# Two scan terms added on GpSimd before TensorE turns them, and a block's experts and biases summed in one PSUM bank

## The chip, the core and the metric

The kernel runs on one core of a Trainium2 chip. The core has five engines, each with an instruction queue of its own that runs in order: TensorE (PE, matmuls; its weight loads are listed apart as PEld), VectorE (DVE), ScalarE (ACT), GpSimd (POOL) and SyncE (SP), which here issues the DMAs of the main part. SBUF is the on-chip memory of 128 partitions; PSUM, in eight banks of 128x512 fp32, is where TensorE writes. The metric is the device time of one execution in microseconds, taken as the median of several runs.

## The reference

Two layers on four images of 128 channels and 64x64 pixels, all in fp32. Layer 0 is a hybrid of a local convolution and a Mamba scan, layer 1 is attention followed by a mixture of experts. The two parts that the change touches, cut to what matters:

```python
# layer 0, per image and channel group; N = 16 states, L = 4096 positions
dA  = jnp.exp(delta[..., None] * A)
dBu = delta[..., None] * Bm[:, :, None, :] * xin[..., None]
def step(h, inp):
    dA_t, dBu_t, C_t = inp
    h = dA_t * h + dBu_t
    y = jnp.einsum('bdn,bn->bd', h, C_t)      # a sum over the 16 states
    return (h, y)
...
y = ys + D_skip * xin
out = y * silu(z) @ out_proj_w.T

# layer 1, mixture of experts: 8 experts, the two best of each token
router_probs = softmax(x @ router_w + router_b)
top_p, top_i = top_k(router_probs, 2); top_p = top_p / sum(top_p)
expert_out = einsum('bnd,edc->bnec', x, expert_w) + expert_b
out = einsum('bnk,bnkc->bnc', top_p, take_along_axis(expert_out, top_i))
t = t + out
```

## The kernel before

An image is cut into 8 blocks of 512 positions, 32 blocks in all (b, i). Everything lies as 128 partitions by 512 positions. The scan of a block runs in two passes (p = 0, 1), each with 128 of the inner channels in the partitions, and a pass in 8 *units* of two states each (n = 0, 2, ... 14): 512 units. One scan instruction of VectorE carries both states of a unit, 1025 columns long.

The main loop (from line 1322) walks through *slots*, two to a unit; `END` is 1024. Its order of calls is the order of every engine's queue: `Queue` and `queued` (lines 450 to 467) chain each instruction behind the one before it on the same engine, which is why nearly all instructions carry line 467 in the profile; tiles tell them apart. What a unit does:

- In its even slot `driven` (line 799) multiplies the unit's B rows, broadcast by DMA from memory (`rows`), with `du` into `h` (VectorE, 128x1024), and `scan` runs the recurrence in place. ScalarE has made the decays `da` in the slots before (`decayed`).
- In its odd slot `read` (line 813) multiplies `h` with the C rows into `hc`, a tile of two buffers, 128x2x512: one half per state.
- The sum over the 16 states is made by TensorE: `turned_on` (line 824) transposes a half in four 128x128 pieces and accumulates into the PSUM tile `y`. The pieces wait in the deque `due` with a slot from which they may go: state 0 from the slot after the readout (three slots after it in the first unit of a pass), state 1 two slots after. They leave in the order in which they came. Behind the last unit of a pass, ScalarE copies `y` out (`yT`), `turned_back` transposes it back in the next slot, and `summed_up` gates it one slot later.

Beside this the loop issues, in every slot, one group of attention: four score matmuls (`sc`, from `attention`), two exponentials of 128x1024 on ScalarE (`pT`, `exponentials`) and, one slot later, eight matmuls with the values (`av`, `weighted`). There are 1024 groups; they begin when the first blocks are through layer 0, and the last of them run after slot 1024.

All other work lies in two *lanes*, X and Y: generators that are moved on by one `yield` twice a slot (`advance`, line 1216). Lane Y holds norms and convolution (`group_norm`, `first_norm`, `conv`; from the second image on the convolution's nine taps are VectorE's) and the projections of `inputs` (line 713). Lane X holds `closed` (the end of layer 0 and the projections of attention) and `finished` (line 1087: the end of attention, the router and the experts of one block). When the scan is over, lane Y takes blocks of `finished` too. Each lane has one PSUM bank, `work(lane)` (line 509). `inputs` uses both banks, and the set `held` with the entry "in" keeps another `inputs` away while it does. If an input is not ready when its rows are due, `until` (line 1246) moves the lanes on until it is.

`finished` computes the router, then `prT`: the eight weights of each token and, below, the same over the norm. For each pair of experts, `share` loads the weights' rows broadcast to all partitions by DMA, VectorE multiplies them with the tokens `xf` (128x1024), and TensorE applies the two experts (`ew`). In the version before, the bias term (`eb8` with `prT`) and each of the four pairs are separate results in the lane's bank, and VectorE adds them one by one into `res`, the first together with `xf`.

GpSimd has little to do: the powers `rs` (an inverse square root of 128x4), the products `shift` behind them, and small fills and copies at the rims of tiles. ScalarE's normalisation `xt` waits for `rs` and `shift`.

Of the kernel before, what the change touches and what calls it, by code (L numbers as in the profile page):

```python
# [24 lines left out]
NST = 16  # L25
DH = 32
NH = 4
NE = 8
# [8 lines left out]
def conv_mamba_attn_moe_kernel(ctx: ExitStack, tc: tile.TileContext, t: dict):  # L37
# [435 lines left out]
    def mm(out, lhsT, rhs, start=True, stop=True):  # L473
        tensor.matmul(out, lhsT=lhsT, rhs=rhs, start=start, stop=stop)
# [8 lines left out]
    def send(out, in_, slots=1):  # L483
        outgoing.append([slots, out, in_])
# [24 lines left out]
    def work(lane, shape=None):  # L509
        return ps_work.tile(shape or [P, BLK], F32, tag=f"work{lane}", name=f"ps_{lane}")  # L510

    def tmp(lane, name, shape=None):
        return side.tile(
            shape or [P, BLK], F32, tag=f"tmp{lane}", name=name, bufs=6 if lane == "X" else 4
        )
# [197 lines left out]
    def inputs(b, i, p):  # L713

        xn, pairs = xn_of[b, i], pairs_of[b, i]
        r = slice(DI * p, DI * p + DI)
        while held:
            yield
            yield
        held.add("in")  # L720
        ps = work("Y")
        summed(ps, [(inxc[:, j, :], pairs[:, p, 2 * j : 2 * j + BLK]) for j in range(2)])
        pz = work("X")
        mm(pz, inz[r, :], xn[r, 3 : 3 + BLK])
        yield
        xin = mix.tile([P, BLK], F32, name="xin", bufs=2)
        scalar.activation(xin, ps, AF.Silu, bias=cb)
        zs = mix.tile([P, BLK], F32, name="zs", bufs=4)
        scalar.activation(zs, pz, AF.Silu)
        yield  # L730

        pb = work("X")
        mm(pb[0:DI, :], wbc, xin)
        ps = work("Y")
        mm(ps, wdt, xin)
        yield
        held.clear()
        bc = tmp("Y", "bc")[0:DI, :]
        scalar.copy(bc, pb[0:DI, :])
        bcd = dram.tile([2, NST // 2, 2, 2 * BLK], F32, name="bcd", bufs=4)  # L740
        send(bcd.rearrange("c n k (m q) -> (c n k m) q", m=2), bc)

        e = tmp("Y", "e")
        scalar.activation(e, ps, AF.Abs, bias=dtb)
        scalar.activation(e, e, AF.Exp, scale=-1.0)
        ln = tmp("Y", "ln")
        scalar.activation(ln, e, AF.Ln, bias=1.0)
        delta = mix.tile([P, BLK], F32, name="delta", bufs=2)
        scalar.activation(delta, ps, AF.Relu, bias=dtb)
        yield  # L750
        yield

        du = mix.tile([P, BLK], F32, name="du", bufs=2)
        lost = du
        vector.tensor_scalar(lost, e, 1.0, -1.0, ALU.add, ALU.add)
        vector.tensor_sub(lost, e, lost)
        vector.tensor_add(ln, ln, lost)
        vector.tensor_add(delta, delta, ln)
        vector.tensor_mul(du, delta, xin)
        in_of[b, i, p] = xin, zs, delta, du, bcd  # L760
        done.add(("in", b, i, p))
        yield
# [324 lines left out]
    def finished(b, qb, lane):  # L1087

        q, u = divmod(qb, 2)
        td = kqv[b][3]  # L1090
        s = slice(qb * BLK, (qb + 1) * BLK)
        acc = side.tile([P, NT, C], F32, name="acc", bufs=2)
        aT, inv = tmp(lane, "aT"), tmp(lane, "inv")
        sync.dma_start(out=aT, in_=total[b, q][u, 0].rearrange("h d q -> (h d) q"))
        sync.dma_start(
            out=inv, in_=inverse[b, q][u][:, None, :].to_broadcast([NH, DH, BLK])
        )
        sync.dma_start(out=acc.rearrange("p j c -> p (j c)"), in_=td[:, s])
        yield
        yield  # L1100
        yield
        vector.tensor_mul(aT, aT, inv)
        yield
        ps = work(lane, [P, NT, C])
        for j in range(NT):
            mm(ps[:, j, :], aT[:, j * P : (j + 1) * P], wp)
        yield
        vector.tensor_add(acc, ps, acc)
        rs = spread(lane, acc)
        yield  # L1110
        ps = transposed(lane, acc)
        yield
        xf = tmp(lane, "xf")
        scalar.copy(xf, ps)
        yield
        ps = work(lane, [P, NT, NE])
        for j in range(NT):
            mm(ps[:, j, :], xf[:, j * P : (j + 1) * P], rw)
        wide = [P, NT, NE]

        def routed(name, n=NE):
            return small.tile([P, NT, n], F32, name=f"{name}{lane}", bufs=1)

        yield

        both = routed("both", 2 * NE)
        pr = routed("pr")
        vector.tensor_mul(pr, ps, rs[:, :, None].to_broadcast(wide))
        vector.tensor_add(pr, pr, rb[:, None, :].to_broadcast(wide))
        m = routed("m", 1)  # L1130
        vector.tensor_reduce(m, pr, AX.X, ALU.max)
        vector.tensor_sub(pr, pr, m.to_broadcast(wide))
        yield
        yield
        scalar.activation(pr, pr, AF.Exp)
        yield
        yield

        revb = rev[:, None, :].to_broadcast(wide)

        def largest(src, tag):
            top, f, pick = routed(f"top{tag}", 1), routed(f"f{tag}", 1), routed(f"pick{tag}")
            vector.tensor_reduce(top, src, AX.X, ALU.max)
            vector.tensor_tensor(pick, src, top.to_broadcast(wide), ALU.is_equal)
            vector.tensor_mul(pick, pick, revb)
            vector.tensor_reduce(f, pick, AX.X, ALU.max)
            vector.tensor_tensor(pick, pick, f.to_broadcast(wide), ALU.is_equal)
            return top, pick

        top1, pick1 = largest(pr, 1)  # L1150
        rest = routed("rest")
        vector.scalar_tensor_tensor(rest, pick1, -2.0, pr, ALU.mult, ALU.add)
        top2, pick2 = largest(rest, 2)
        vector.tensor_add(pick1, pick1, pick2)
        vector.tensor_mul(pr, pr, pick1)
        vector.tensor_add(top1, top1, top2)
        vector.reciprocal(top1, top1)
        vector.tensor_mul(both[:, :, 0:NE], pr, top1.to_broadcast(wide))
        vector.tensor_mul(both[:, :, NE:], both[:, :, 0:NE], rs[:, :, None].to_broadcast(wide))
        yield  # L1160

        ps = work(lane)
        for j in range(NT):
            tensor.transpose(ps[0 : 2 * NE, j * P : (j + 1) * P], both[:, j, :], ident)
        yield
        prT = tmp(lane, "prT")[0 : 2 * NE, :]
        scalar.copy(prT, ps[0 : 2 * NE, :])
        shares = dram.tile([NE, BLK], F32, name=f"shares{lane}")
        send(shares, prT[NE:, :])
        yield  # L1170

        def share(e):

            if lane == "X":
                w = side.tile([P, 2, BLK], F32, name="share", bufs=3)
            else:
                w = mix.tile([P, 2, BLK], F32, tag="rows", name="share", bufs=4)
            sync.dma_start(
                out=w.rearrange("p k q -> p (k q)"),
                in_=shares[e : e + 2].rearrange("e q -> (e q)")[None].to_broadcast([P, 2 * BLK]),  # L1180
            )
            return w


        ps = work(lane)
        mm(ps, eb8, prT[0:NE, :])
        yield
        res = tmp(lane, "res")
        vector.tensor_add(res, ps, xf)
        yield  # L1190
        ahead = deque(share(e) for e in (0, 2))
        yield
        yield
        for e in range(0, NE, 2):
            if e + 4 < NE:
                ahead.append(share(e + 4))
            yield
            w = ahead.popleft()
            if e:
                vector.tensor_add(res, res, ps)  # L1200
            vector.tensor_mul(w, w, xf[:, None, :].to_broadcast([P, 2, BLK]))
            yield
            ps = work(lane)
            for u in range(2):
                mm(ps, ew[:, e + u, :], w[:, u, :], u == 0, u == 1)
        yield
        vector.tensor_add(res, res, ps)
        send(out[b][:, s], res, 2)
        yield


# [86 lines left out]
    groups = attention_groups()  # L1298
    units = [(b, i, p, n) for b, i in blocks for p in range(2) for n in range(0, NST, 2)]
    END = 2 * len(units)  # L1300

    rows, due, closing, y_of = {}, deque(), deque(), {}
    h_of, slot = {}, 0
# [18 lines left out]
    while (  # L1322
# [23 lines left out]
        if unit and odd:  # L1346
            hc = read(h, rows.pop((at, 1)))
            late = 2 * (unit[3] == 0)
            due.append((slot + 1 + late, unit, 0, hc[:, 0, :], False))
            due.append((slot + 2, unit, 1, hc[:, 1, :], ends(unit)))  # L1350
        advance("Y", False)
        while closing and closing[0][0] <= slot:
            summing = turned_back(*closing.popleft()[1:])
# [133 lines left out]
```

## Time and profile before

| what | us |
|---|---|
| median of three runs | 5234.72 (5234.31 to 5243.44) |
| the profiled execution, whole | 5221.24 |
| its span, first to last instruction | 5219.4 |
| PE busy | 4743.5 (91%) |
| PEld busy | 2300.7 (44%) |
| DVE busy | 3834.5 (73%) |
| ACT busy | 3749.8 (72%) |
| POOL busy | 423.5 (8%) |
| mean granted TensorE clock | 0.958 of full speed |

Busy time is the time in which an engine ran at least one instruction, with register, branch, semaphore and DMA-issuing instructions left out. Over the whole span it mixes three phases: a start in which the first blocks go through layer 0, a long middle in which scan and attention run side by side, and an end in which attention and experts of the last image are left. A line of the groups reads: source line, engine, operation, out<-in by the program's names, shapes, count, then busy time in us and mean ns of one, then idle time of the engine just before them and what ended it. A line of the timeline reads: start, length, engine, line, operation, names, shapes, count.

The chain of work that ended last, followed back from the last instruction, shares the span like this: PE 55%, DVE 18%, ACT 13%, DMA 6%, issue 5%, POOL 2%; its largest single parts are `av` on PE with 23%, `sc` on PE with 13%, the experts' `ps_X` on PE with 8%, `h` on DVE with 6%, and `y` on PE with 5%.

### The profile page before, as it was taken

How to read it: one execution, taken by the hardware profiler on the slowest of the kernel's cores; microseconds unless marked ns; L12 is line 12 of the kernel's file. 1: busy time of each engine (PE TensorE's matmuls, PEld its weight loads, DVE VectorE, ACT ScalarE, POOL GpSimd, SP SyncE). 2: the span in 40 equal slices, each digit the busy share in tenths (PEclk: the TensorE clock that was granted, in tenths of full speed). 3: DMA queues.
4: the chain of work that ended last, by engine and by line, in shares of the span. 5: the costliest groups of instructions: out<-in, count | busy, mean ns of one | idle time of the engine just before them, and what ended most of it. 6: DMA issues, size and time to landing. Idle time of an engine off the chain costs nothing.

```text
span 5219.4 us, 62693 instructions
## 1 busy us (share of the span) xinstructions
PE 4743.5 (91%) x20704; PEld 2300.7 (44%) x20704; DVE 3834.5 (73%) x5809; ACT 3749.8 (72%) x5701; POOL 423.5 (8%) x483
## 2 busy tenths in 40 slices
PE   4566898999999999899999999999999999999997
PEld 2333444444444444444444444444444444443443
DVE  4888767777788877888788877888788877751332
ACT  3456787788777777688887787788777787756543
POOL 1111101100000000001000000000000001000000
PEclk8677999999999999899999999999999999999998
DMA  3556667767776667767766667767766666754542
GB/s 96 188 186 202 206 215 247 232 231 238 244 231 218 227 227 243 238 232 246 260 230 231 224 223 230 262 227 259 259 236 227 215 230 226 263 181 153 184 134 72
DMA packets 451694, 1131.62 MB, mean 217 GB/s; under 512 B 51985, under 2 KB 135330, under 8 KB 451362
## 3 DMA queue, kind: packets, MB, share of 16 engines
q1 hardware_dynamic: 450194, 1126.74, 64.3%
q8 instruction: 166, 2.72, 0.2%
q14 instruction: 166, 1.36, 0.1%
q10 hardware_dynamic: 1168, 0.80, 0.1%
HBM read 967.12 MB, written 143.39 MB: 213 GB/s over the span
## 4 chain that ended last, share of the span: by engine, by line
PE 55%; DVE 18%; ACT 13%; DMA 6%; issue 5%; POOL 2%; SPq 1%; DVEq 0%; ACTq 0%; POOLq 0%
PE av L467 23%; PE sc L467 13%; PE ps_X L467 8%; DVE h L467 6%; PE ps_Y L467 5%; PE y L467 5%; ACT pT L467 4%; ACT L467 3%; DMA ks<-kd 2%; DVE hc L467 2%; ACT xt L467 1%; ACT e L467 1%; DMA rows<-bcd 1%; DVE stX L467 1%; POOL rsX L467 1%
## 5 line engine op out<-in xcount | busy, mean ns | idle before, releaser
L467 ACT ACTIVATE pT<-sc 128x1024 f32<-128x1024 f32 x2048 | 1984.8, 1023 | 940.1 <-PE sc L467 938.4
L467 PE MATMUL av<-pT,v 128*64 128x512 f32 x8192 | 1998.3, 609 | 12.4 <-DVE avs L467 12.4
L467 PE MATMUL sc<-qs,ks 128*128 128x512 f32 x4096 | 1296.1, 436 | 64.4 <-DMA ks<-kd 32.7
L467 DVE TENSOR_TENSOR_SCAN h<-da,state,h 128x1025 f32<-128x1025 f32 x512 | 1204.2, 2352 | 90.0 <-ACT h L467 56.2
L467 PEld LDWEIGHTS sc<-qs,ks 128*128 128x128 f32 x4096 | 701.3, 190 | 793.3 <-ACT pT L467 261.7
L467 PEld LDWEIGHTS av<-pT,v 128*64 128x64 f32 x8192 | 499.5, 137 | 844.4 <-issue 813.8
L467 ACT ACTIVATE da<-delta,amat 128x512 f32<-128x512 f32 x1024 | 743.0, 730 | 1.9
L467 PE MATMUL y<-ident,hc 128*128 128x128 f32 x4096 | 626.6, 284 | 64.9 <-DVE hc L467 64.9
L467 DVE TENSOR_TENSOR hc<-rows,h 128x1024 f32<-128x1024 f32 x512 | 624.2, 1219 | 16.1 <-PE y L467 5.9
L467 DVE TENSOR_TENSOR h<-rows,du 128x1024 f32<-128x1024 f32 x512 | 623.4, 1218 | 14.2 <-DMA rows<-bcd 13.7
L467 PEld LDWEIGHTS y<-ident,hc 128*128 128x128 f32 x4096 | 520.6, 147 | 235.7 <-issue 83.9
L467 ACT ACT_TABLE_LOAD x319 | 409.3, 1283 | 19.5 <-DVE zs L467 14.3
L467 POOL TENSOR_TENSOR rsX<-rsX,mhalf 128x4 f32<-128x4 f32 x92 | 203.8, 2216 | 2524.6 <-DVE rsX L467 2440.5
L467 POOL TENSOR_TENSOR rsY<-rsY,mhalf 128x4 f32<-128x4 f32 x100 | 130.4, 1304 | 2071.0 <-DVE shiftY L467 1560.3
L467 DVE TENSOR_TENSOR avs<-av,prev 128x512 f32<-128x512 f32 x96 | 66.1, 689 | 252.9 <-PE av L467 238.3
L467 PE MATMUL ps_X<-share,w_ew 128*128 128x512 f32 x432 | 215.5, 622 | 8.7 <-DVE share L467 8.5
L467 ACT ACTIVATE xt<-ps_Y,shiftY,rsY 128x128 f32<-128x128 f32 x380 | 143.8, 469 | 106.4 <-POOL shiftY L467 99.0
L467 DVE TENSOR_TENSOR share<-share,xf 128x1024 f32<-128x1024 f32 x128 | 155.9, 1218 | 15.6 <-DMA share<-sharesX 9.9
L467 ACT COPY state<-h 128x2 f32<-128x2 f32 x448 | 88.7, 198 | 93.5 <-DVE h L467 93.5
L467 DVE SCALAR_TENSOR_TENSOR cm<-y,w_fc1w,cm 128x512 f32<-128x512 f32 x192 | 142.8, 744 | 3.4
L467 PE MATMUL ps_Y<-pairs,inxc 128*128 128x512 f32 x256 | 129.2, 629 | 15.6 <-DMA pairs<-xn 10.3
L467 PEld LDWEIGHTS ps_X<-share,w_ew 128*128 128x128 f32 x432 | 73.6, 190 | 146.8 <-issue 98.5
(254 smaller groups left out, 3455.8 us busy)
## 6 DMA issues: line engine op xcount, KB each, us to landing
rows<-bcd SPq DMA_DIRECT2D x1024, 512.0 KB
ks<-kd SPq DMA_DIRECT2D x192, 512.0 KB
qs<-qd SPq DMA_DIRECT2D x161, 512.0 KB
share<-sharesX SPq DMA_DIRECT2D x108, 512.0 KB
v<-vd SPq DMA_DIRECT2D x192, 256.0 KB
ks<-kd SPq DMA_DIRECT2D x128, 256.0 KB
avd<-avs SPq DMA_DIRECT2D x96, 256.0 KB
prev<-avd SPq DMA_DIRECT2D x96, 256.0 KB
```

The costliest lines, as they stand in the source:

```text
L467: return lambda *args, **kw: queued(op(*args, **kw))
```

## The change

Two parts.

**The scan's terms.** From slot `ALONE` on (64, the end of the second block), GpSimd adds the two halves of `hc` in place, right behind `read` in the order of issue, and one group of four transposes turns the sum into `y`, two slots after the readout (three in the first unit of a pass). Before slot 64 all stays as it was.

**The experts.** `finished` no longer adds each result on VectorE. The bias matmul opens an accumulation in the lane's bank just ahead of the first pair of experts, the eight expert matmuls go on in the same bank, and one addition at the end makes `res` from it and `xf`. Since the bank of lane X is now in use from the first pair to the last, `finished` in lane X waits while `held` is not empty, and then enters "mix", which keeps `inputs` away until `res` is made.

```diff
--- before.py
+++ after.py
@@ -734,7 +734,7 @@
         ps = work("Y")
         mm(ps, wdt, xin)
         yield
-        held.clear()
+        held.discard("in")
         bc = tmp("Y", "bc")[0:DI, :]
         scalar.copy(bc, pb[0:DI, :])
         bcd = dram.tile([2, NST // 2, 2, 2 * BLK], F32, name="bcd", bufs=4)
@@ -1182,30 +1182,34 @@
             return w
 
 
-        ps = work(lane)
-        mm(ps, eb8, prT[0:NE, :])
-        yield
-        res = tmp(lane, "res")
-        vector.tensor_add(res, ps, xf)
+        yield
         yield
         ahead = deque(share(e) for e in (0, 2))
         yield
         yield
+        while lane == "X" and held:
+            yield
+            yield
+        if lane == "X":
+            held.add("mix")
+        ps = None
         for e in range(0, NE, 2):
             if e + 4 < NE:
                 ahead.append(share(e + 4))
             yield
             w = ahead.popleft()
-            if e:
-                vector.tensor_add(res, res, ps)
             vector.tensor_mul(w, w, xf[:, None, :].to_broadcast([P, 2, BLK]))
             yield
-            ps = work(lane)
+            if e == 0:
+                ps = work(lane)
+                mm(ps, eb8, prT[0:NE, :], True, False)
             for u in range(2):
-                mm(ps, ew[:, e + u, :], w[:, u, :], u == 0, u == 1)
-        yield
-        vector.tensor_add(res, res, ps)
+                mm(ps, ew[:, e + u, :], w[:, u, :], False, e + u == NE - 1)
+        yield
+        res = tmp(lane, "res")
+        vector.tensor_add(res, ps, xf)
         send(out[b][:, s], res, 2)
+        held.discard("mix")
         yield
 
 
@@ -1298,6 +1302,7 @@
     groups = attention_groups()
     units = [(b, i, p, n) for b, i in blocks for p in range(2) for n in range(0, NST, 2)]
     END = 2 * len(units)
+    ALONE = NB // 2 * NST
 
     rows, due, closing, y_of = {}, deque(), deque(), {}
     h_of, slot = {}, 0
@@ -1346,8 +1351,12 @@
         if unit and odd:
             hc = read(h, rows.pop((at, 1)))
             late = 2 * (unit[3] == 0)
-            due.append((slot + 1 + late, unit, 0, hc[:, 0, :], False))
-            due.append((slot + 2, unit, 1, hc[:, 1, :], ends(unit)))
+            if slot < ALONE:
+                due.append((slot + 1 + late, unit, 0, hc[:, 0, :], False))
+                due.append((slot + 2, unit, 1, hc[:, 1, :], ends(unit)))
+            else:
+                gpsimd.tensor_add(hc[:, 0, :], hc[:, 0, :], hc[:, 1, :])
+                due.append((slot + 2 + late // 2, unit, 0, hc[:, 0, :], ends(unit)))
         advance("Y", False)
         while closing and closing[0][0] <= slot:
             summing = turned_back(*closing.popleft()[1:])
```

## The prediction

> **What bounds the kernel now.** I read the busy time by stretches first, then the groups, then the waits, then the order of time. The 1024 slots of the scan begin at about 100 us and their last readout starts at 4608 us; the 33rd of the 512 readouts (slot 64, from where the change adds) starts at 316 us. So three stretches matter (columns: length, then PE, PEld, DVE, ACT, POOL busy, granted clock, DMA share, GB/s):
>
> ```profile
> core 0: us, PE busy (x) PEld busy (x) DVE busy (x) ACT busy (x) POOL busy (x), PEclk, DMA share, GB/s
> 310.00:520.00 210.00, 144.03 (x559) 77.27 (x559) 175.12 (x236) 119.43 (x220) 26.13 (x26) 0.80 0.59 198
> 520.00:4600.00 4080.00, 3862.55 (x17302) 1880.81 (x17303) 3262.27 (x4739) 3186.23 (x4877) 350.04 (x381) 0.98 0.70 235
> 4600.00:5219.00 619.00, 576.22 (x2284) 246.07 (x2280) 177.10 (x470) 308.63 (x345) 12.61 (x13) 0.96 0.42 140
> ```
>
> TensorE is busy 95% of the middle stretch (3863 of 4080), VectorE 80%, ScalarE 78%. Before 520 us attention has hardly begun and VectorE leads (175 of 210); after 4600 us TensorE alone finishes the last image. The waits agree: the engines behind TensorE wait for it, and it waits little (us in total, times, longest).
>
> ```profile
> ACT pT L467 <- PE sc L467: 938.4, 661, 9.5
> DVE avs L467 <- PE av L467: 238.3, 62, 17.3
> PE y L467 <- DVE hc L467: 64.9, 21, 9.0
> ```
>
> The groups that the change touches (busy us, mean ns of one, idle before):
>
> ```profile
> L467 PE MATMUL y<-ident,hc 128*128 128x128 f32 x4096 | 626.6, 284 | 64.9 <-DVE hc L467 64.9
> L467 DVE TENSOR_TENSOR hc<-rows,h 128x1024 f32<-128x1024 f32 x512 | 624.2, 1219 | 16.1 <-PE y L467 5.9
> L467 DVE TENSOR_TENSOR h<-rows,du 128x1024 f32<-128x1024 f32 x512 | 623.4, 1218 | 14.2 <-DMA rows<-bcd 13.7
> L467 DVE TENSOR_TENSOR res<-res,ps_X 128x512 f32<-128x512 f32 x108 | 73.7, 682 | 51.9 <-PE ps_X L467 51.5
> ```
>
> Before its 512 `h` products VectorE idles 14.2 us in all: each starts right behind whatever went before, so a delay there is passed on until VectorE next idles, before `avs` for example.
>
> **Transposes removed.** Of 512 units 480 lose one of two groups of four transposes: 1920 instructions. What a group takes of TensorE's order:
>
> ```profile
> 2511.45 1.47 PE L467 MATMUL y<-ident,hc 128*128 128x128 f32 x12
> 2512.85 1.94 PE L467 MATMUL av<-pT,v 128*64 128x512 f32 x8
> ...
> 2515.75 0.60 PE L467 MATMUL y<-ident,hc 128*128 128x128 f32 x4
> 2516.28 1.94 PE L467 MATMUL av<-pT,v 128*64 128x512 f32 x8
> ```
>
> Four of them move `av` back by 2516.28 - 2515.75 = 0.53 us; twelve take 1.40, so 0.47 for four; by busy time it is 4 x 626.6/4096 = 0.61. I take 0.53, the group as it stands between two others, and keep 0.47 and 0.61. The middle stretch holds 449 readouts (29 fall before 520 us, 2 after 4600), so TensorE sheds 449 x 0.53 = 238 us there.
>
> **GpSimd's additions.** 480 of them, 128x512, two inputs in SBUF. No row shows this form. The nearest (minimum/median/maximum ns):
>
> ```profile
> L467 POOL TENSOR_TENSOR shiftY<-shiftY,rsY x95: 200/249/1910, 43.6 to 4408.5; 128x4 f32<-128x4 f32 x95
> L467 POOL COPY y<-y x28: 235/240/1155, 50.2 to 4224.3; 128x64 f32<-128x64 f32 x28
> L467 POOL COPY xn<-xn x28: 180/182/2246, 156.4 to 4409.6; 128x3 f32<-128x3 f32 x28
> ```
>
> From 3 to 64 columns a copy grows by 55 ns, 0.90 ns a column. Below: the fill of a 128x512 tile, `vst`, takes 0.54 us and reads nothing. Above: 235 ns for 64 columns, taken as all columns, makes 1.88 us for 512. Between, nearest in kind: 180 + 2 x 0.90 x 509 = 1.10 us, the copy's slope once for each input; I take that. POOL then works 480 x 1.10 = 528 us more and, 8% busy now, has room.
>
> The price is on VectorE. The maxima above are not work:
>
> ```profile
> 886.03 2.34 DVE L467 TENSOR_TENSOR_SCAN h<-da,state,h 128x1025 f32<-128x1025 f32 x1
> 886.45 1.91 POOL L467 TENSOR_TENSOR shiftY<-shiftY,rsY 128x4 f32<-128x4 f32 x1
> ```
>
> The shift product of 0.20 us, started inside the scan, ends at 888.36, as the scan does at 888.37: GpSimd is shut out while VectorE reads two operands from SBUF. No row shows the reverse, since its present operands are four columns. Lower bound of VectorE's loss per addition: 0; upper: the whole addition, 1.88. I take exclusion as mutual, so VectorE loses 1.10 where such an operation stands right behind the readout. Followed through VectorE's order from 470 us on, that is so behind 392 of 459 readouts (0.85), mostly the next unit's `h` product or a convolution tap; behind the others it idles or reads PSUM. Mean loss 0.85 x 1.10 = 0.94 us per unit.
>
> The Trainium skill, SBUF — State Buffer, section "SBUF: two separate sides", calls the port pair of VectorE and GpSimd an exclusive lock held for a whole instruction; the scan's row agrees for one direction, and by it the sum would be the one taken here. The rule against this change is in GPSIMD Engine Reference, "Engine selection": two-input elementwise work belongs on VectorE, GpSimd being 1.96 times slower. On a row of 0.69 us for a 128x512 product that is an estimate of 1.36 us, and by it the kernel would gain about 10 us only.
>
> **Waits added.** An addition waits for the readout; behind it on POOL stand the `rs` powers and `shift` products that ScalarE's `xt` waits for. TensorE waits for `xt` 22 times before a matmul; an addition is ahead or running for about 2.2 of the 9.1 us of a unit (4080/449), so 22 x 0.24 x 1.10 = 6 us; bounds 0 and 22 x 1.10 = 24. TensorE's own wait for the sum costs nothing: the group stands one slot (4.5 us) later than the first group did, which covers POOL's 1.10 and up to 2.35 behind a scan. Without that cover it would be those 3.45 us at each of the 21 waits shown, 72 us. For the first unit of a pass it stands as before, three slots behind the readout. The `hc` buffer comes free in the same slot as before.
>
> **Experts in one bank.** Four of five `res` additions per block go: 128 x 0.69 = 88 us of VectorE, some 60 of it before 4600 us (22 of 32 blocks), 1.0 us per 68 us; the ten later blocks find VectorE 71% idle: nothing. The bias matmul moves by some four slots, and shares, loads and yields stay in number and place. The hold: counted through the code's yields, a block's mixing lies at slots 11 to 17 of its 32, the input projections at 3 and 24 or, in an image's last block, 19; they touch once. Where they would meet, the input has three slots to spare. Zero; with that cover gone, one bunching of some slots, say 10 to 20 us.
>
> **Sum.** Cutting 520 to 4600 us into sixty stretches of 68 us and adding up the busiest engine of each gives 3871 us, 0.949 of the time; TensorE leads in 58. Per stretch (7.5 units) TensorE's work shrinks by 4.0 and VectorE's time grows by 7.5 x 0.94 - 1.0 = 6.0. Two of them:
>
> ```profile
> 2356.00:2424.00 68.00, 66.30 (x306) 31.84 (x304) 54.93 (x79) 58.53 (x91) 7.48 (x7) 1.00 0.79 263
> 3036.00:3104.00 68.00, 65.75 (x306) 32.47 (x304) 64.29 (x119) 49.77 (x83) 9.78 (x14) 1.00 0.68 229
> ```
>
> become 62.3 against 60.9, and 61.8 against 70.3, where VectorE takes over. It leads in 29 of the sixty; the maxima add up to 3765, at 0.949 that is 3968: -112 us. Before 520 us, where VectorE leads, 29 x 0.94 = +27. With POOL's +6: **-79 us**. The profiled execution (5219.4 us span, 5221.2 in all) becomes 5142; the median of the runs is 13.5 higher, so **5156 us**.
>
> **Rivals.**
> 1. *VectorE isn't held up*: lower bound of the loss, 0 to 0.46 per unit (an addition of 0.54). The maxima add up to 3650 to 3695, -233 to -186 in the middle, with the early cost -233 to -173, down to -263 at 0.61 a group: 4972 to 5062. For it: only POOL is seen waiting. Against: a shared path should stop either.
> 2. *VectorE becomes the bound, and it is slower*: the price is the addition's hold on VectorE behind the readout. With the early units the sum is zero at a loss of 1.2 us a unit, an addition of 1.4. At 1.60 (1.88 x 0.85) it is +104 in the middle and +46 early: 5385. For it: VectorE already leads in two stretches and readouts are followed at once; against: the copy's slope is far below.
> 3. *No effect*: the transposes hid under waits that stay. Against: TensorE idles 5%. It would end within 10 us, about 5235.
>
> **Chances.** Forecast (0.46 to 1.15 lost a unit, 5060 to 5220) 0.50; rival 1 0.20; rival 2 0.22; rival 3 0.08. A measurement of this kernel tells about 0.2% (10 us) from no change: faster 0.70, same 0.08, slower 0.22. The range runs from 4985, most of rival 1, to 5270, the cheap part of rival 2. The forecast's own is 5060 to 5220.
>
> **What would show it.** 2176 `y` transposes of `hc`, some 333 us busy; a POOL group `hc` of 480, near 1.1 us where VectorE idles, longer behind a scan; `h`, scan or the next product late or longer by about 1 us behind readouts; 32 `res` additions; TensorE below 93% of the middle stretch. I am wrong if an addition takes 1.4 us or more of VectorE, or if its rows don't move at all.

## The result, and the profile after

The changed kernel takes 5249.7 us (median of 20 runs, 5235.7 to 5254.8), the kernel before beside it 5238.4 (5231.5 to 5249.8): a ratio of 1.0021, 95% interval 1.0014 to 1.0028. The forecast was 5156, with its own range at 5060 to 5220; the change is 11 us slower, and all that it was to save is gone. The profiled execution has a span of 5246.9 us, 27.5 more than before. The stretches that the prediction used, in the kernel after (length, then PE, PEld, DVE, ACT, POOL busy, granted clock, DMA share, GB/s; the last one is 27 us longer than before):

```profile
310.00:520.00 210.00, 126.02 (x428) 63.10 (x426) 188.95 (x234) 113.36 (x209) 74.22 (x53) 0.75 0.59 196
520.00:4600.00 4080.00, 3722.92 (x15400) 1687.02 (x15396) 3456.60 (x4613) 3176.91 (x4858) 1178.64 (x826) 0.96 0.70 233
4600.00:5246.00 646.00, 602.09 (x2410) 257.68 (x2408) 181.02 (x472) 330.78 (x377) 30.88 (x23) 0.97 0.43 146
```

TensorE is busy 91% of the middle instead of 95%, VectorE 85% instead of 80%, and the scan is no faster: its last readout starts at 4642 us instead of 4608. The scan's group on the page before, then the groups of the page after (busy us, mean ns of one, idle before):

```profile
L467 DVE TENSOR_TENSOR_SCAN h<-da,state,h 128x1025 f32<-128x1025 f32 x512 | 1204.2, 2352 | 90.0 <-ACT h L467 56.2
```

```profile
L467 PE MATMUL av<-pT,v 128*64 128x512 f32 x8192 | 2018.3, 614 | 25.4 <-DVE avs L467 25.0
L467 PE MATMUL sc<-qs,ks 128*128 128x512 f32 x4096 | 1320.1, 442 | 125.4 <-ACT pT L467 66.6
L467 POOL TENSOR_TENSOR hc<-hc 128x512 f32<-128x512 f32 x480 | 826.7, 1722 | 2352.1 <-DVE hc L467 2164.0
L467 DVE TENSOR_TENSOR_SCAN h<-da,state,h 128x1025 f32<-128x1025 f32 x512 | 1339.3, 2616 | 68.8 <-ACT h L467 33.9
L467 DVE TENSOR_TENSOR h<-rows,du 128x1024 f32<-128x1024 f32 x512 | 700.6, 1368 | 7.3 <-DMA rows<-bcd 7.2
L467 PE MATMUL y<-ident,hc 128*128 128x128 f32 x2176 | 354.8, 292 | 55.0 <-DVE hc L467 36.9
```

The change does what it says: 2176 transposes instead of 4096, 480 additions on GpSimd. The scan's mean went from 2352 to 2616 ns and the `h` product's from 1218 to 1368, though they compute what they did. The order of time of VectorE and GpSimd shows how:

```profile
3029.37 1.22 DVE L467 TENSOR_TENSOR h<-rows,du 128x1024 f32<-128x1024 f32 x1
3029.53 2.19 POOL L467 TENSOR_TENSOR hc<-hc 128x512 f32<-128x512 f32 x1 [3.66 <-DVE hc L467]
3030.69 3.18 DVE L467 TENSOR_TENSOR_SCAN h<-da,state,h 128x1025 f32<-128x1025 f32 x1
...
3051.09 1.35 POOL L467 TENSOR_TENSOR hc<-hc 128x512 f32<-128x512 f32 x1
3051.41 1.59 DVE L467 TENSOR_TENSOR ln<-ln,du 128x512 f32<-128x512 f32 x1
```

The first addition starts 0.16 us into the `h` product and takes 2.19 us, where the shortest of the 480 takes 1.255: it ends 1.13 us behind the product's end at 3030.59, as if it had hardly begun before. The scan, which starts 0.1 us behind that end, takes 0.83 us more than its 2.35. At 3051 a product of 0.69 us takes 1.59. Each engine holds the other up, as the prediction assumed. And TensorE's waits, two of the kernel before and then those after (us, times, longest); before, it also waited 45.9 us for `bothX` and 32.7 for `ks`:

```profile
PE ps_Y L467 <- ACT xt L467: 71.3, 22, 7.7
PE sc L467 <- ACT pT L467: 30.5, 91, 1.6
```

```profile
PE ps_Y L467 <- ACT xt L467: 87.8, 56, 7.7
PE ps_X L467 <- DVE bothX L467: 74.9, 27, 6.6
PE sc L467 <- ACT pT L467: 66.6, 156, 2.6
PE sc L467 <- DMA ks<-kd: 56.4, 24, 9.3
```

No new wait dominates; many small ones grew. Where the 27.5 us come from, with each moment of TensorE's order put down to the matmul that started last: `hc` transposes 566 to 318 us (-248), all other matmuls 4178 to 4295 (+117), idle 476 to 634 (+159).

### The profile page after: what moved, and what is told of

The parts are those of the page before. It is cut to its first block, busy times and chain, and to the rows that moved or that the text cites. A ratio compares the mean times of both kernels' runs of the same rounds, so it can differ in the third digit from the quotient of the medians.

```text
span 5246.9 us, 59811 instructions
## 1 busy us (share of the span) xinstructions
PE 4612.4 (88%) x18784; PEld 2103.2 (40%) x18784; DVE 4044.0 (77%) x5681; ACT 3756.0 (72%) x5701; POOL 1318.5 (25%) x963
## 4 chain that ended last, share of the span: by engine, by line
PE 41%; DVE 28%; ACT 13%; DMA 7%; issue 7%; POOL 2%; SPq 1%; DVEq 0%; ACTq 0%; POOLq 0%
PE av L467 17%; DVE h L467 12%; PE sc L467 10%; PE ps_X L467 6%; PE ps_Y L467 5%; ACT pT L467 4%; ACT L467 3%; DVE hc L467 3%; DMA ks<-kd 3%; PE y L467 2%; DVE cm L467 2%; ACT xt L467 2%; DMA rows<-bcd 1%; DVE stY L467 1%; DVE stX L467 1%
## 5 line engine op out<-in xcount | busy, mean ns | idle before, releaser
L467 PE MATMUL sc<-qs,ks 128*128 128x512 f32 x4096 | 1320.1, 442 | 125.4 <-ACT pT L467 66.6
L467 POOL TENSOR_TENSOR hc<-hc 128x512 f32<-128x512 f32 x480 | 826.7, 1722 | 2352.1 <-DVE hc L467 2164.0
L467 DVE TENSOR_TENSOR_SCAN h<-da,state,h 128x1025 f32<-128x1025 f32 x512 | 1339.3, 2616 | 68.8 <-ACT h L467 33.9
L467 PEld LDWEIGHTS sc<-qs,ks 128*128 128x128 f32 x4096 | 712.5, 193 | 876.4 <-ACT pT L467 388.1
L467 DVE TENSOR_TENSOR h<-rows,du 128x1024 f32<-128x1024 f32 x512 | 700.6, 1368 | 7.3 <-DMA rows<-bcd 7.2
L467 PE MATMUL y<-ident,hc 128*128 128x128 f32 x2176 | 354.8, 292 | 55.0 <-DVE hc L467 36.9
L467 PEld LDWEIGHTS y<-ident,hc 128*128 128x128 f32 x2176 | 292.4, 152 | 167.7 <-issue 61.0
L467 DVE SCALAR_TENSOR_TENSOR cm<-y,w_fc1w,cm 128x512 f32<-128x512 f32 x192 | 185.7, 967 | 3.4
L467 PE MATMUL ps_Y<-ident,xt 128*128 128x128 f32 x380 | 72.3, 322 | 87.9 <-ACT xt L467 87.8
```

Source lines behind the costliest of these rows:

```text
L467: return lambda *args, **kw: queued(op(*args, **kw))
```

## The experiments

Ratios are to the kernel before in the same comparison, with 95% intervals. Its medians there lie between 5234 and 5242 us, so a few us between two tables say nothing. Kernels that leave a term out, or count it twice, serve to measure alone.

**First set: the scan's part, taken apart.** Two by two: four or eight transposes a unit, with and without the addition, experts as before.

`e1_half_turned`, no addition, four transposes:

```diff
-                gpsimd.tensor_add(hc[:, 0, :], hc[:, 0, :], hc[:, 1, :])
                 due.append((slot + 2 + late // 2, unit, 0, hc[:, 0, :], ends(unit)))
```

> The scan part of the change without GpSimd's addition: from slot 64 on one group of four transposes a unit turns state 0 alone, so the second state of 480 units is left out of the sum; experts as before the change. Theory A (the transposes were worth their TensorE time, and the addition's hold on VectorE gives it back): 180 to 260 us below the kernel before, VectorE's scan back at 2352 ns mean. Theory B (the transposes were not on the path, something else paces the slots): less than 60 us below. Theory C (TensorE's clock falls when it has less to do and eats the gain): less than 100 us below, with a granted clock clearly under 0.95.

`e2_late_group`, no addition, eight transposes in one later group:

```diff
-                gpsimd.tensor_add(hc[:, 0, :], hc[:, 0, :], hc[:, 1, :])
-                due.append((slot + 2 + late // 2, unit, 0, hc[:, 0, :], ends(unit)))
+                due.append((slot + 2 + late // 2, unit, 0, hc[:, 0, :], False))
+                due.append((slot + 2 + late // 2, unit, 1, hc[:, 1, :], ends(unit)))
```

> Both states are turned as before, eight transposes a unit, but in one group at the later slot; no addition, experts as before. All theories that blame the addition: within 15 us of the kernel before. A rival (turning one slot later, in one lump, costs by itself): more than 25 us above.

`e3_turn_both`, `e2` with the addition kept:

```diff
+                gpsimd.tensor_add(hc[:, 0, :], hc[:, 0, :], hc[:, 1, :])
                 due.append((slot + 2 + late // 2, unit, 0, hc[:, 0, :], False))
                 due.append((slot + 2 + late // 2, unit, 1, hc[:, 1, :], ends(unit)))
```

> GpSimd adds as in the change, but both halves are turned in one late group of eight, so state 1 of 480 units is counted twice; experts as before. What the addition alone costs, against the kernel with the late group. Theory A: 150 to 260 us above it. Theory B (TensorE is not the bound, VectorE is hidden too): under 60 us above it.

`e4_terms_only`, the change without its edits to `inputs` and `finished`; on the changed kernel, in short:

```diff
-                mm(ps, eb8, prT[0:NE, :], True, False)
...
+                vector.tensor_add(res, res, ps)
```

> The scan part of the change alone, experts as before the change. If the experts' part brings what it takes off VectorE's path: 10 to 60 us above the changed kernel. If the experts' bank is what costs (the accumulation over five slots, the hold): below the changed kernel by 30 us or more.

| kernel | median us | ratio |
|---|---|---|
| e1 no addition, four | 5138.4 | 0.9817 (0.9788 to 0.9846) |
| e2 no addition, eight, late | 5218.9 | 0.9970 (0.9957 to 0.9982) |
| e3 addition, eight, late | 5366.6 | 1.0254 (1.0223 to 1.0285) |
| e4 addition, four | 5295.6 | 1.0118 (1.0086 to 1.0150) |

The addition costs 148 us beside eight transposes (e3 - e2) and 157 beside four (e4 - e1). Four transposes less bring 81 us (e2 - e1) and 71 (e4 against e3). The late group alone brings 18, slightly beyond its expected 15. The experts' part, as the changed kernel against e4, brings 46, within the 10 to 60 expected. So theory A holds for the price of the addition (148 is just under its 150) and fails for the transposes: e1 lies 99 us below the kernel before, where A asked for 180 to 260. B asked for less than 60, C for less than 100 at a clock clearly under 0.95; e1's clock is 0.950, against 0.955 in e2. None fits whole. The page lines of TensorE in e2 and in e1:

```profile
PE 4740.6 (91%) x20704; PEld 2302.3 (44%) x20704; DVE 3835.0 (74%) x5809; ACT 3748.7 (72%) x5701; POOL 420.0 (8%) x483
```

```profile
PE 4573.9 (89%) x18784; PEld 2087.4 (41%) x18784; DVE 3834.1 (75%) x5809; ACT 3749.5 (73%) x5701; POOL 423.7 (8%) x483
```

Put down as above, from e2 to e1 the `hc` transposes lose 219 us (533 to 314), the other matmuls gain 52 (4207 to 4260) and idle gains 79 (475 to 555): 88 us of span. Of the 52, the clock may explain some 26: the time lost to a granted clock under 1.0 goes from 233 to 259 us; the rest is open. The idle time is in many waits that grow. TensorE's two for a score matmul are shown, first in e2 and then in e1; its waits for `xt` go from 69 to 77 us, for `bothX` from 47 to 55 and for `share` from 9 to 18:

```profile
PE sc L467 <- ACT pT L467: 34.1, 90, 2.1
PE sc L467 <- DMA ks<-kd: 42.8, 16, 8.8
```

```profile
PE sc L467 <- ACT pT L467: 61.5, 156, 2.6
PE sc L467 <- DMA ks<-kd: 53.7, 25, 9.2
```

TensorE's order of time in e1 shows the worth of one group and two of the waits:

```profile
2505.09 0.73 PE L467 MATMUL sc<-qs,ks 128*128 128x512 f32 x2 [1.69 <-ACT pT L467]
...
2513.18 1.16 PE L467 MATMUL sc<-qs,ks 128*128 128x512 f32 x4 [1.15 <-DMA ks<-kd]
...
2516.57 1.20 PE L467 MATMUL sc<-qs,ks 128*128 128x512 f32 x4
2517.70 1.94 PE L467 MATMUL av<-pT,v 128*64 128x512 f32 x8
2519.56 1.19 PE L467 MATMUL sc<-qs,ks 128*128 128x512 f32 x4
2520.60 0.60 PE L467 MATMUL y<-ident,hc 128*128 128x128 f32 x4
2521.12 1.94 PE L467 MATMUL av<-pT,v 128*64 128x512 f32 x8
```

From `sc` to `av` it takes 1.56 us with a group between (2519.56 to 2521.12) and 1.13 without (2516.57 to 2517.70): a group is worth 0.43 us, not 0.53, because without it the last score matmul takes longer until its follower starts. The medians over the middle of e1 are 1.56 (261 cases) and 1.13 (162). 480 groups make 207 us, an estimate.

**Second set: the experts' part, VectorE's addition, a higher dose.** `e5_experts_only` is the change without its edits to the main loop:

```diff
-            if slot < ALONE:
...
-                gpsimd.tensor_add(hc[:, 0, :], hc[:, 0, :], hc[:, 1, :])
-                due.append((slot + 2 + late // 2, unit, 0, hc[:, 0, :], ends(unit)))
```

> The experts' part alone, the scan's terms turned as before the change. Theory A (VectorE's time counts only where VectorE sets the pace, which without GpSimd's additions is seldom): 10 to 35 us below the kernel before, less than the 46 us it brought beside the additions. Rival (the additions to res stood on the block's own chain, so it brings the same everywhere): 40 to 55 us below. Rival (the bank held through five slots costs): not below.

`e6_experts_late` is the changed kernel with the diff of `e2`, `e7_vector_adds` the changed kernel with this:

```diff
-                gpsimd.tensor_add(hc[:, 0, :], hc[:, 0, :], hc[:, 1, :])
+                vector.tensor_add(hc[:, 0, :], hc[:, 0, :], hc[:, 1, :])
```

> The experts' part and one late group of eight transposes, no addition on GpSimd. If the parts add up: 18 us (the late group) plus what the experts' part alone brings, so 30 to 60 us below the kernel before and about 45 to 75 us below the changed one.

> The changed kernel with the addition of the two terms on VectorE in place of GpSimd: 480 x 0.69 us = 331 us of VectorE's own time in place of 285 us of stretched instructions, and no lock. Theory A (what counts is VectorE's lost time, whoever takes it): within 45 us of the changed kernel, rather above. Rival (GpSimd's lateness at TensorE and ScalarE is what costs): 60 us or more below the changed kernel.

`e8_few_turned`, on `e1`:

```diff
-                due.append((slot + 2 + late // 2, unit, 0, hc[:, 0, :], ends(unit)))
+                if unit[3] == 0 or ends(unit):
+                    due.append((slot + 2 + late // 2, unit, 0, hc[:, 0, :], ends(unit)))
```

> As the kernel that turns state 0 alone, and besides no group is turned for the six middle units of each pass, so 360 of 480 units are left out of the sum: 360 x 0.43 us = 155 us less of TensorE. Theory D (TensorE is the pace and its clock or issue took the rest): 120 us or more below the kernel that turns state 0 alone. Theory E (beyond the first tens of us ScalarE's exponentials, the lanes' chains and the loads pace the slots, so TensorE's time counts by some 40%): 40 to 80 us below it, with TensorE's idle time up by 70 us or more. Theory F (nothing more to gain): within 20 us.

| kernel | median us | ratio |
|---|---|---|
| e5 experts only | 5231.8 | 1.0000 (0.9990 to 1.0009) |
| e6 experts and late group | 5222.3 | 0.9973 (0.9963 to 0.9983) |
| e7 additions on VectorE | 5239.7 | 1.0008 (0.9999 to 1.0017) |
| e8 few units turned | 5098.7 | 0.9744 (0.9729 to 0.9758) |

Alone the experts' part brings nothing that can be measured, less than expected: 77 us less of VectorE's busy time (3834.5 to 3758) do not show where VectorE is not tight. No run takes them apart from the bank that is held longer. Beside the additions the same edit brought 46. e6 lies about 14 us below the kernel before, where 30 to 60 were expected, and 27 below the changed one, where 45 to 75 were: again the experts' part adds nothing to the late group. The additions on VectorE itself are at least as good as on GpSimd (5239.7 against 5249.7), within the 45 us of theory A though not above: VectorE's lost time counts, whoever takes it. e8 fits theory E, at its lower edge: an estimated 155 us less of TensorE bring 40, and idle time grows by 99 (555 to 654). Its granted clock is 0.942, against 0.955 in e2.

**Third set: what holds VectorE, and a better version.** `e9_half_experts` is the changed kernel with the diff of `e1`, that is `e1` with the experts' part:

> State 0 alone is turned from slot 64 on (the second state of 480 units is left out), without GpSimd's addition, and the experts are summed in one bank. Theory G (with TensorE relieved VectorE is the next to set the pace): the experts' part, worth 2 us alone and 46 beside the additions, brings 25 us or more below the kernel that turns state 0 alone with the old experts. Theory H (VectorE becomes the pace only through the additions; what is left is chains between engines): within 15 us of it.

`e10_fill_only` and `e11_one_read`, on `e2`, in front of its first `due.append`:

```diff
+                gpsimd.memset(hc[:, 0, :], 0.0)                              # e10
+                gpsimd.tensor_scalar_mul(hc[:, 0, :], hc[:, 0, :], 2.0)     # e11
```

> The kernel with the late group of eight, and in place of the addition a fill of the first half of hc with zeros by GpSimd (480 times, writes only, so state 0 of 480 units is left out of the sum). If GpSimd and VectorE exclude each other over reading: VectorE's scan and h product at their old means, 2352 and 1218 ns, and the time within 15 us of the late group's. If any GpSimd instruction on 512 columns holds VectorE: 60 us or more above it.

> The same with GpSimd doubling the first half of hc in place (one input of 512 columns read, so state 0 of 480 units counts twice). If VectorE is held while GpSimd reads: half the reading of the addition, some 0.45 us per held instruction, 100 to 190 us of stretched VectorE instructions in all, and 50 to 95 us above the late group, half of what the addition cost. If only two inputs collide: within 15 us of the late group.

`e12_chosen_units`, on the changed kernel:

```diff
-            else:
+            elif at % 16 in (1, 11, 12):
                 gpsimd.tensor_add(hc[:, 0, :], hc[:, 0, :], hc[:, 1, :])
                 due.append((slot + 2 + late // 2, unit, 0, hc[:, 0, :], ends(unit)))
+            else:
+                due.append((slot + 2 + late // 2, unit, 0, hc[:, 0, :], False))
+                due.append((slot + 2 + late // 2, unit, 1, hc[:, 1, :], ends(unit)))
```

> Experts in one bank, and GpSimd adds only in the units 1, 11 and 12 of each 16, 90 of them, where in the changed kernel VectorE was held in 7 to 27% of the cases; all other units are turned in one late group of eight. If the addition's price is where it falls: 90 x 0.17 us = 15 us of TensorE's groups realised and some 10 us lost to VectorE, so 0 to 15 us below the kernel with experts and late group alone (5222). If its price is the same everywhere: 90 x 0.31 = 28 us lost against 15, so 5 to 20 us above it.

| kernel | median us | ratio |
|---|---|---|
| e9 four transposes, no addition, experts | 5120.0 | 0.9773 (0.9755 to 0.9792) |
| e10 fill in place of the addition | 5220.5 | 0.9966 (0.9952 to 0.9979) |
| e11 one input read | 5257.6 | 1.0042 (1.0026 to 1.0057) |
| e12 additions in chosen units | 5206.9 | 0.9943 (0.9924 to 0.9961) |

e9 lies 18 us below e1, between what G and H asked for: undecided. It lies 102 us below e6, from which it differs by the four transposes alone, so with the experts' part in place they bring 102 rather than 81, and the addition costs 130 (5249.7 against e9). In e10 GpSimd fills 480 times and nothing stretches; in e11 it reads one input, and the scan's mean rises by 54 ns. The first two lines are of e10, the others of e11:

```profile
L467 DVE TENSOR_TENSOR_SCAN h<-da,state,h 128x1025 f32<-128x1025 f32 x512 | 1204.3, 2352 | 94.9 <-ACT h L467 60.0 <-DVE h L467 2.3
L467 POOL MEMSET hc<- 128x512 f32 x480 | 262.4, 547 | 2810.1 <-DVE hc L467 2598.9 <-PE av L467 94.8 <-PE ps_X L467 53.1
```

```profile
L467 DVE TENSOR_TENSOR_SCAN h<-da,state,h 128x1025 f32<-128x1025 f32 x512 | 1231.8, 2406 | 86.2 <-ACT h L467 51.5 <-DVE h L467 2.3
L467 POOL TENSOR_SCALAR hc<-hc 128x512 f32<-128x512 f32 x480 | 926.2, 1930 | 2326.3 <-DVE hc L467 1990.7 <-PE av L467 96.0 <-PE sc L467 92.7
```

So GpSimd's reading holds VectorE, its writing does not. The Trainium skill, SBUF — State Buffer, "Who interferes with whom", says just that of VectorE instructions with two SBUF inputs; e10 agrees with 0 us stretched. That the loser is blocked for the whole instruction, as the same page's "SBUF: two separate sides" has it, e11 contradicts: an instruction of 1.49 us (its minimum) stretches most scans that it meets by 0.16 to 0.32 us and most `h` products by 0.41. One multiplication runs from 3015.67 to 3018.00 us; the scan that starts at 3016.76, inside it, takes 2.51 us, 0.16 more than its 2.35. All VectorE instructions together are stretched by 68 us where 100 to 190 were expected, and it costs 39 us against e2, where 50 to 95 were.

e12, which computes the whole sum, is faster than both kernels, 0.9943 of the one before, and 15 us below e6, at the edge of the 0 to 15 expected where the price depends on where an addition falls. Its 90 additions stretch VectorE's instructions by some 22 us in all (busy 3778.7 us, 3757.1 in e6).

**Fourth set: does one engine hold the freed TensorE?** The pair e2 and e1 again, once with ScalarE relieved, once with VectorE:

```diff
+            if slot < ALONE:                                                  # e13, e14
-            decayed(units[ahead], decays[ahead % 2], k)
+                decayed(units[ahead], decays[ahead % 2], k)
...
-            else:                                                             # e15, e16
-                vector.scalar_tensor_tensor(hr, y0, w, hr, ALU.mult, ALU.add)
```

> The late group of eight, with ScalarE's 960 decay exponentials from slot 64 on left out (the scan goes on with the decays of the last units before), some 700 us of ScalarE's time. The base for the next run. If ScalarE helps to set the pace already: 40 us or more below the late group (5219); otherwise within 30 us.

> The same with state 0 alone turned (second state of 480 units left out). TensorE sheds 207 us; with ScalarE at its old load 81 of it came out. Theory I (the score matmuls wait for ScalarE's exponentials, that took the rest): 130 us or more below the run before it. Theory J (ScalarE isn't what holds them): 60 to 100 us below it.

> The late group of eight, with eight of the nine convolution taps of images 1 to 3 left out on VectorE, 192 x 0.74 = 143 us. The base for the next run. If TensorE sets the pace there: within 30 us of the late group (5219); if VectorE does in these stretches: 60 us or more below.

> The same with state 0 alone turned. Theory G (VectorE takes over as TensorE is relieved): 110 us or more below the run before it, where it was 81 with all taps. Theory H (chains between engines, wherever the work lies): 70 to 95 us below it.

| pair | eight transposes | four | four less bring |
|---|---|---|---|
| as they were (e2, e1) | 5218.9 | 5138.4 | 81 |
| ScalarE relieved (e13, e14) | 5203.1, 0.9928 (0.9907 to 0.9949) | 5110.9, 0.9754 (0.9738 to 0.9771) | 92 |
| VectorE relieved (e15, e16) | 5193.3, 0.9917 (0.9901 to 0.9934) | 5091.6, 0.9727 (0.9708 to 0.9745) | 102 |

Relieving an engine alone brings 16 us (e13) and 26 (e15) against e2, both within the 30 allowed for an engine that does not set the pace. ScalarE's busy time falls by 580 us (3749 to 3169, less than the 700 expected), and the transposes bring 92: theory J. With the taps gone they bring 102, between the 95 of H and the 110 of G. From the ratios' intervals each of the three differences is known to some 13 to 17 us, so 81, 92 and 102 can hardly be told apart. Neither engine alone lets the 207 us out.

## Why the prediction was wrong, point by point

**The step that failed** is the one from TensorE's time to the kernel's. The prediction put it so: "TensorE sheds 449 x 0.53 = 238 us there", and "the maxima add up to 3765, at 0.949 that is 3968"; without a loss on VectorE the same step gave -233. It took TensorE's share of idle time as fixed and TensorE as the pace wherever it is the busiest. Measured without the addition, the transposes with their later place bring 99 us (e1), of which 81 come from the four left out. Of the 219 us by which the transposes' share of the order shrinks, 79 become idle time, 52 go into slower matmuls, and 88 come out of the span. A further dose brings only 40 of an estimated 155. The sizes were not what failed: 0.43 us for a group and a loss of 0.61 us a unit, both measured, give -110 us in the prediction's own sum. TensorE was busy 95% of a stretch and waited for by the others, but its own instructions have other waits close behind, and these grow as it gets ahead: of the score matmuls for `pT` and the keys' loads, of the lanes' matmuls for `xt`, `bothX` and `share`. Which of these chains costs how much is not settled: two of the engines, relieved singly, did not change the answer by more than 21 us. Most signs that the prediction named came true (2176 transposes, 355 us busy, 32 `res` additions, TensorE at 91% of the middle, `h` products longer by 1.08 us, the median, where an addition held them): they show the parts and not this step.

**The group's size**, 0.53 us, was 0.43, just under the lower bound of 0.47; the follower's start was counted, not what the score matmul ahead gives up.

**The addition.** 1.10 us was forecast, 1.255 is its minimum. VectorE was to lose 0.94 us per unit; its instructions are stretched by 293 us, 0.61 for each of the 480, and 347 additions (0.72, where 0.85 was put) run beside a stretched one. The forecast price of that loss, from -233 to -85, is 148 us; 148 and 157 were measured, 130 with the experts' part in place. The price was about right by luck: with the 0.61 the prediction's sum would have made it 83, so each microsecond lost cost more than the sixty stretches made of it.

**Waits.** TensorE's waits for `xt` rose from 71 to 88 us, +17 where +6 was put, within the 24 allowed. For the sum itself TensorE waited 3 times, 17.9 us, where nothing was put, and 28 us less than before for the readout. The late group cost nothing, as forecast, and brings 18 us, which was not. The 33rd readout starts at 310 us, not at 316; nothing rests on it.

**The experts' part** was worth 1.0 us a stretch on VectorE: nothing alone (e5), 46 us where the additions make VectorE tight. That the hold costs nothing is not shown by itself; hold and saving together came to nothing in e5.

**Put together**: -18 for the late group, -81 for the transposes, +157 for the addition, -46 for the experts make +12; measured are +11. It must be so, since each run (e2, e1, e4) is one step further from the one kernel to the other. By another way (e2, e6, e9) it is -18, about +3 for the experts, -102 and +130. The forecast was -79. Rival 2 named the engine that the saving goes to, and its range holds the measured time, but it asked for a loss of 1.2 us or more a unit; at 0.61 VectorE eats more than the transposes bring because they bring so little. Rival 3 came near in time, for a reason that does not hold: the transposes hide only in part.

## What to carry to other kernels

- Busy share says who is waited for, not what a cut is worth. Before a microsecond off the busiest engine is booked as gained, leave its work out and time that: one run (e1, or e9 with the experts' part) shows the most that the idea can bring.
- An elementwise operation on GpSimd was not free for VectorE here when both read SBUF; put it only where VectorE reads PSUM or idles (e12), and look for stretched instructions, not for waits, to find its price.
- The same edit can be worth nothing or 46 us, depending on whether the engine that it relieves is tight; measure parts of a change apart and together.

## What the runs showed of the hardware

TensorE's granted clock is lower in those of these kernels in which TensorE waits much more. The records hold only 1.0 and 0.5, in pieces of 3 us and longer; over the whole span the time lost at 0.5, half of its length, is 233 us in e2, 259 in e1, 294 in e8 and 298 in the changed kernel, against 218 before, while idle time goes 475, 555, 654, 634 and 476. Work taken off TensorE thus went with a slower rest of its work. The Trainium skill, TensorE: Matmul & The Clock Gate, "HAM oscillation — how this bites in real kernels", describes such a fall to half rate behind idle gaps; the pieces of half clock here agree: between 520 and 4600 us of e1, TensorE was busy 34% of the 3.4 us ahead of such a piece (median of 37), against 93% over the whole stretch. The page's rule speaks of gaps longer than about 3.4 us; here 32 of the 37 pieces had no gap between matmuls that long in the 13 us ahead, so shorter gaps, close together, were enough.

GpSimd's hold on VectorE depends on the operation, not on its length: where they meet, the two-input addition of 1.255 us stretches most scans by 0.81 to 0.98 us and most `h` products by 0.46 to 1.09, the one-input multiplication of 1.49 us by 0.16 to 0.32 and 0.41 (shortest times; e11 for the multiplication), and the fill of 0.52 us neither (e10).
